# Two-layer hybrid block: gate logits from the attention product and from x, norm factors in the rows, gathers that add to the residual

## The chip, the cores and the metric

The kernel runs on one core of a Trainium2 chip. The metric is the device time of one launch in microseconds. Three runs of the kernel before took 533.31, 535.4 and 535.91 us, the median is 535.4. One more execution was taken with the hardware profiler; it is the source of every row shown below.

The engines have short names here. PE is the matrix engine (TensorE), and PEld its weight loads, which overlap the products. DVE is VectorE, ACT is ScalarE, POOL is GpSimd, and SP is SyncE, which issues most of the plain transfers. SBUF is the on-chip memory that all of them read, PSUM the accumulators that PE writes, DRAM the memory outside.

## The reference

The input is x, 16 sequences of 256 tokens with 128 features, 4096 tokens in all. Four sublayers add to it, each on a layer norm of x without scale or shift:

```python
x = x + attn_a(layernorm(x), ...)      # attention whose softmax is summed out
x = x + ffn(layernorm(x), gate_w, w1, w2)      # layer 1 of the experts
x = x + attn_b(layernorm(x), ...)      # selective scan
x = x + ffn(layernorm(x), gate_w, w1, w2)      # layer 2 of the experts
```

The first sublayer multiplies the softmax, summed over the axis along which it adds to one, by v of the same token. What remains is a linear map: v's projection, then the output projection, both with a bias.

The expert sublayer is a mixture of 8 experts. Each token takes the two with the largest gate logits (`x @ gate_w`), weighted by a softmax over these two logits; an expert is two products, 128 to 512 and back, with a relu between.

The selective scan has 16 states; it is computed for the last 180 tokens of a sequence and fewer for the faster states, and a test at the end of the kernel falls back to a general path where that would not be enough. The same test looks for experts that got more tokens than they have room for.

## The kernel before

**Tiles and stages.** Tokens are cut into 8 blocks of 512, each as four tiles of 128 tokens by 128 features (`x{b}`, tokens on partitions). Layer 1 takes the blocks in the sets [0], [1], [2, 3], [4, 5], [6, 7], layer 2 in the sets [0, 1], [2, 3], [4, 5], [6], [7]. For every set, `layer` (L1476) calls what comes before the experts (`attention`, L1024, in layer 1, `gate`, L1047, in layer 2), then `route` (L1139), then `experts` (L1189), then what comes behind (`arrive`, L1456, with the scan `mixer`, or `finish`, L1464, which writes the output).

**Attention and gate.** `attention` loads a block of the transposed input, transposes it on PE, copies it from PSUM to SBUF as x, takes mean and variance with `bn_stats` (`statistics`, L999), and adds the bias `batt` to x. The product of the transposed input with `wat` (the two projections in one, centred so that the mean drops out) is multiplied by the reciprocal deviation and added to x. Then `gate` takes statistics of the new x, normalizes it into `xn` (`normalize`, L1007), transposes `xn`, copies it from PSUM into `xnT`, multiplies each of its four tiles by the 8 gate columns `gw_s`, and copies the logits out. `rstd_of` (L978) works out the reciprocal deviation with a power on POOL and one correction step on DVE.

**Routing.** `choose` (L1063) finds the two largest logits of each token and their weights `p`. `route` counts, with short bf16 products, which place each token gets in its expert's list, writes a row `xn * p` for each of the two experts (relu and both products are positively homogeneous, so the weight can go in first), and scatters the rows with indirect transfers from POOL to `slots` in DRAM: 8 scatters of 128 rows for a block.

**Experts.** SP fetches an expert's rows (`xs`), PE transposes them, multiplies by `w1_s`, ACT or DVE take the relu (`h`), PE multiplies by `w2_s` (`ps_y`), the result is copied out (`yr`) and SP stores it to `ys` in DRAM. When all experts of a set are stored, `collect` (L1244) gathers for each tile its two rows by indirect transfers from POOL (`gather`, L866) into buffers `yy`, and DVE or POOL add them to x, 512 columns at a time.

**The order of the work.** All of this is first recorded as jobs (`Plan`), not issued. Each job has its possible engines and an assumed duration on each, an assumed time from issue to landing for transfers (`late`), and what it has to follow. `forward` (L299) walks through the jobs and gives each an engine and a place; a long string, `ORDER` (L50), holds the rank of every job and decides between those that are ready. The engines then get their instructions in that order, and each works through its own queue without overtaking. Where the walk leaves PE without work for half a microsecond or more, `tile_layers` puts filler products in (L1502, blank by ones, one per 0.26 us of assumed idle), which keep PE running. Between two scatters that go out one behind the other, POOL gets a small memset (L1508).

**Buffers.** PSUM has three one-bank buffers of the kind `b`, one of the kind `y` and two of two banks each of the kind `B` (`BANKS`, L48). In SBUF there are three buffers for the transposed input (`load_x`, L890), four for `xn`, three for rows and for `yy`. A reused buffer makes its next writer wait for its last reader.

In the profile, nearly every instruction has the line of one helper (L758, L752 in the changed kernel), so rows are told apart by the tiles that they name. Names in the profile leave out buffer numbers: `w_s` stands for `w1_s` and `w2_s`, `ps_b`, `ps_B` and `ps_y` for the PSUM buffers.

Of the kernel before, what the change touches and what calls it, by code (L numbers as in the profile page):

```python
# [19 lines left out]
P = 128  # L20
# [26 lines left out]
XN, ROW, XS, XT, H, YT, DEPTH = 4, 3, 4, 3, 4, 3, 3  # L47
# [3 lines left out]
    "c-lo*30#cp_kWj}DT#_AT7*zhQ6XChm91pS7A2IZi(Fe$gsvjHEQye<l%>^jvxkHdDbb>klt|mmyvzTbXS%<?d}iL6d7kr}^F815"  # L51
    "J?HU#VARmG%HBTCvo=}ry|n&yah-awiDRP9k+c_yjPV!WH?lfzanRb9_sVr|zjr;?vNb8P(*i|bF9&N++nrCm`^1`9mTCDLP(jsB"
    "akkpxLeF5E+<(H1gO}BR9C$XlUUA{epZqIz;hjflbGO<Wduz6~R2xewC3*Sgs~4>D>6&)gV94nOVcNnjhx$=(!^GzB!pI;03<_?R"
    "b!ah4eU<OA=EaTGQA>B^tzCM2dQh_KrJijwlKU0NO=o@&Nmq-lq<-2z2`f&H>b7HNp{;{FZO-eT7PY$`*$n=ir9n5ES-L%RE;mT1"
    "r+ewI2<#P;+?^ZNmd0j>1zyoPF|u;%Turs4g&7BijhVE}vB@npbge<&h_>mIJY^yJ*;a*5|4KKjIBV0jLqv$|ZQ|T#LDn%x3x9e4"
    ")vcl|DCecx=RWosPIG)als&WDIN{k5+3?db&K_F)sW0n{`$WdQ`SHtS|K1bnwnMikTOOaOvAsmlu|1U>;$7g^{p_#iW9GFhs0a2R"
    "y3a8>w?|uZ--f*j22;4Ov{}w3CqGnMg*0_osn>grZ{~B;{Y%!JzjMke;=bN)M{ic`=CMOVqutlp+JAfSw?%nccCWchmlzvGzgB3@"
    "ao#A~wDSJO`?Ed$D=((U%&*YxD!n$Y&l<nlaD%Iwo2%*h9XHIG^5OE$DWAtUd2~Ok@DG-B({;G8%jk*2-u;85vqx5$PQ7R`qs1$>"
    "CaAk%*pF=`M=$J*ZoF;xD#ALtX|S%%5YwSYA|i*DKEAvB$5EG<F|VwwLfbTsuFo!C((})Yl6!G)Hl-i`x+*5CT)WMrN^M%Qo9z9W"
    ">@-@t*g`lsXtuA>`o3naXO7dc$palSQwRFaS#%-t-uJHGyr!JfPs|J){jaC<!mKqByC)cIOlU1zXzua&hQrEuf1ln{-xtJ8DP8zp"  # L60
    "C*k(vUhLzSJKS#mEaaEA4YONPpr1f*t(^P(U|FE%r)XVw_3${~P_2HOcAB{jNiyoa=ic!`+bu`aPkpwq>^RH&)w4TO$4pGxc)hgW"
    "&u+yj)ZEgXolS>&jJrOxsO9OJ#L>QU!-Ll9jp!XWgBiPW-EP-&h1!)CLE|zq9`knEV=Jk*y!zz(%kxEAFRM=5c>I&6P2JX=k6(Fq"
    "WXaBZE}a9)BTl>P4?dDTVNk)%z`G_J<4upIrLA86B{m^`^Oe0$AD*7-blL1lOYV$MeeCkb&l%;qa&e8taoehK6Z#FBGym-4Gs}-^"
    "DE>~g9q}#x_qyqkLQ9Zy+SJLF%4E+`W5yPF?V9jsby>jsih7$d^GCgwm5#F4kqxmGww1h{mVHR<u1@W*n(H%e{G4-3DYL0U@#rhR"
    "FMAiP<pvps%=%u*w{jzw$a2?ZFLjB_A7VFpci7>jDLx-B-guL1n^!f*Z_s<!hvq)!q3eTVvtBL?Ut!@FKcuE*tkvlcgYRs)8+>ix"
    "%fq__53RRh`tQcJzBP8%a?zf6t|T|L_wba&DVd#D<a#;FrqAx{cy8N+Z<XB}ateQ6S!}AUKJ0Vj)*S0(n=Xc*uJ}Ivvt|GHV~I6d"
    "f_?D4^QC*IPrqgO)Q6q+rf$zI`y+l|M>m)Zyp-%VZE0TqGLKE#gI-x4JbAVu+rPpz;!MZ4<_As>SNxNF+A=6vGg)vwulB;D?@LX`"
    "^^<PvS-dyXdKm1!y{fQ}XJYD#x~SNO-S3JT9S+R3t~q9KcC+uSp9!(bPE&K7%CvrrEg7bK^KERHEJLuF(P`(u3j$M?)Zg9KYV!PE"
    "eyII1N^OyEj%Bs^zySdVe<#Ldu82NSeE-4li%m8zZ&%zf`8V5w3RLS7(iZbO>uec4&9m6it;i?IHP0tl$s8ZsDQndpbJsCLF17@j"
    "&0F8#H@mJ^Y|NKEGrpD&JKKx4(5bjJ$=vu-mb<~>GwN2((Z!LQ2Da874UN9v*?*5+*>KmaS!~cD9V_#ynB`yVUH^^tIG0zhZEZ3o"  # L70
    "XR@OHm)vaYqOuC#O|KjbuWre?mOr;^op;5kqDdP}y?XuhKC3zNj65t{cV|;vNmk&t34;5c7WXbk?nUV68TnjtoDqJiLRRGybn{_g"
    "p!d1$7Za|Jt9UJELtZt{8jv|^sFmY=>kMYm`vmU;#r6B2`^i#v`Jb@8<?3DjspD_mjKXW3dK!id6|1f8>se+N1@?K=cYwB4&&7wC"
    "-Ziqng6|i2a0?6MzI!*`4|_OlWAd)I>2_7s!HV$KZ~L4ajumKKogd-$@kY_4kO{rG5C49ONKU%_YpP8xr>=Kpq>-O(^xxOYhpioB"
    "-S&0lp~+U)?7|b)WX^rNAm-BNXQw>}UQKA4v}*m&IVFRgex7VtI^+%GEneZC=U#R&iE8X?@Nkj!uWQMpQnnon?lhMl@nvA=0?Tou"
    "mkrysCuDbzyo2+m8*R_6+&k0yRll(|v0~qvhw=J07NgA07~gOlZL`|!)U!(0#w~P*{jvxBC*BIWdpdbykdV-9Ve8bXpUmc|U(&qJ"
    "cMc>atsJp#K|{FShZg1HFS;QHZ8~|wUM>B0!8zI8Cb~5)gWFL%JM2}%_N+aBPRzX|7L<oR87^DzX%}PZ=yb|=^wKclMRxYMUYo1N"
    "1rKoPaCqp#nX7DLKc%#!YEmxal43Ux+4Pr@H=nDixUlGJVRD9Jzfp-!zeX&PJel?;q*Aj^ck<Dr@-L$XuW__monF%6?{3BZtF+d0"
    "HzQmGyW4pi%a)aDey+0ZaroDU1KR`Y6Z75OGOi?5<QnVNZU~4vdul?(wfd3w)QzX^GkEe&Z;5j8R@(vBdx_^Zn07a<=|6}ITBy-$"
    "*P>)Clgk<dO?!qd-m+vFeNH^<wje!<ayq!&_hih4?B+M4?9Np0jnJv~xIXUg<aqaw`EIn8#fvTGW|>~|I&A9jr1s#1VTsqZ(yq-`"
    "UZb3Bdz&y{-YQF1J$&^}wzee4!=Q_vv}2UxZ4>XNFpE?1@ACqZ-aM~<t*iCKIc$-y1~t?tBf=(WMv43P<h4Vj8{Ql<kd?8kQa`M|"  # L80
    "qc5i%O`mxgIb0Y}tl?dt7I(vMmRpJ6tYeXR-F7Wo+qL_>G2dzDWu}vjhgJn#(_XuxJjy@!?=|MV^cMC1vaW~E&EqeP=Et5)dHUAx"
    "<jv&ICXX6A<#1LTR_ron<U0Nh>(W1H+z8z?GT!>l3+vyZRv9DuPwStSbtwKzLTc;0u*s>POz6KO-7S~TsfmiZon?^lyROug>MAb3"
    "`)TL*SNYci$G6#xZ|<G+Bfh?G%~K77!Y*4<?QQCpg~Z2Byr7)w^7_i?+v)KUdp0b*U;X@;euZi2n0r?XJ~)^UpC`;-sj;kkD)Zw0"
    "#hzEPTl2Q8wYha$UcMzhApH1F`o_SiFWRoyM(%$6aB|_44JFmFgMN1F;+_0tXh0|H_aC=T9@AWDQnmQujQr}&UzOUg3WG&O!O`=r"
    "i7Vn_=7nVbe8i66qBEGEA>mfv8*788mnCvG^j%`Nnipl!FRI4$Tix?w=ElJEjsJM{*wo=pNa^TpiJJ5t&x4EC*Ur_odGaIj$<5^W"
    "Tf)k}$LhDPjM!xO?w?`dpT;lD+FM)rqqElgVb%r9J-@B1@hm7bHG0?m?x7*`7d_JM-B%jX9DVWHj)k>{AL?}e<=ybU?=AT~zt<zX"
    "S?x+u*Elq@<EI7gD}T)%8}Mptx0B)Vjb?QN_UOHcO8pjf$?95qL64sYPgJ~&Sdm|}Jih*;sif4|`-H=k=WB9`9cO;r;o7^luv_|r"
    "Qg%4!-#SezVb*TF=^=UV)(kuNk5)as%4oM@-QmKcjSd$zKAf-Y5K^FCbZ_ms#_CyHYoeFk=|AM0-L#ZRllHwcsu|PdcChfc_M`hc"
    "&tKP@Wv`tbDgF21(v>-JC7xSDdsNCE_x#E=@D3iSL)jMpsk4Uc_c}28*|XLr>RrIrjkNIypR@y);(J~mIjS}>%<EUY{@z2hcQzAe"
    "?-c3a)3xwp%6RYHrzbVWwLMc;pO|^pG3&^LJHmeR+P&xYXGVQJpStzA!{y+*BWgLa^!$;cCapP~ODU?`d@s|n(ICFR^_`FYo+HQa"  # L90
    "%{`=u$#t1{+vrz7&Az<UnIE#xzZkUJCHZ2MtnAjoC5>ZZol~jrW)>P|wjmE54Yw<){k&OjuBY9U$)+|xbUYFDgAR6`a^dkj!=zH~"
    "?(Kh)r=2tGsJDOPC$|B9*X{dF?kQxsSKO9Ad{=&CT<E;zW7ki8IpdmT?hUVw@&)e#AHOj)?)x}un)UL^jXGDG1IpyLZapcT+&X{h"
    "k*1~x?rO2UB1{*YZT%i}XlUTG_|KO%7#_CtTs41SMww5n_nXmQGj3k^{&L^sG-LU7dGxV?m7^bgnX&nZ|I1*LDu(IwD9rv@$TrXH"
    "w>d@UX9z}C8fjjuM}MC><zsKbzR$Yw?1?Tpr(;I){(-eeoBKb>?WdvJ=vGsdG@#kJCdKetzZKK}@yR*7tw#Uul|B7$e)bI9Tj??F"
    "^3UygON{=C)7%r_nyrkzo?;wvM!Jse^MF4vvTBwV<zjluFK}7IRp0ZH3pXyU{nM=UXe&$Wa>6@kmA}WXZ&wy9i@R%d;#X=``o!Xf"
    "1!*7O9ZRcNpLzPMTWp6(J(jqC9ud0FN5iW*wQ1baZkMvI4xc%t`|!}*o*tPWz9v<;|2kEEv3qVruZF4y?cO8I4h2v;vFfp-j{NoY"
    "smx$dT6EEx&9BufZmw_r*^RE=+`m^!n-iz|ai>XGw~cvGkuLX#{F#zFyJxFL{}y8t-!!9`X5(*M(S-y>=<^Ns-Gg1;)jeq1T6<%{"
    "hVV}MGp`==_nLGvTDaf!+uT7Xj2}3Aosl2@Qryu@y3K20q*Gz%hlb^^5{B&l**D)UFmT)MTtn$TY2?b=Yh3lO)tz3mi@l|F%-il@"
    "{*~PeI<mD*<-OyJxj*^mFTbol^TOyyw}75|28Hca|NWq$r(Vurt4D3$%NF(9{>SF^`^K5Zp=w_aJIDL(vvV4o_|mdTx64<L@aGqg"
    "c)lo#3|juSA}gQT;o{N7_kKm*ysDOoi4V`;bEj<kYc~ISdC(<hLFX;EFK_FjTfZj9JoNXVXO;FpFR1IBk}dXLG<VeEJkQ3f%f9Wr"  # L100
    "JzL*DVB^g=`+c(>Etq9m;IKR@u18qcE)F9Oy4|z<#N0Y@p^xs?yStvxPh&RFUs5ce1@81NxOnPP^X1uXP2-=P(QTS<o!IAFpLLft"
    "J1i4-I?JZ*DEhWv8g;3*rOYtZ(0A@lxlO@1?;`$d?xrL2G-F1n7kT$M-KqAD&42{I%SCYmEl-_ky1urmZnssbWyg5~bW)a-e;wTM"
    "h=re6TQba|e$t-<cSU>o8(+HED|Nb{`T4a>KmS8U+{eX2nb*JPZBpgwM&;8_YMZQGv?_o37^68eM$P>(*lx{*=A9qU(v5H5=vgn("
    "F{~5&^0Y!!S9Gk`smq^azsO&{$y>XK{!#8UME-c9_my+CPUUvr7fL!UyBQl-c5=4)<81}=FR_<i8}`}%P2cZ*msy`|RyOR*&FJ*m"
    "TP>(4x>rtzP0YR#n`N_BXBO`YQy*DfxnFT-cOT<LpCtWl-m|i$vs@IW*RBtG^l9W4Rw2*dal)xA`kvyQK}`IUT8g4XN~G~c<VA|%"
    "D4JnKhT|C}e8jKe2l7H5sP+e%qG=vJ2xJL^->QD3(3l|7_ys(WAIKJ}eU0h`mkF?l5e1fq(?tQd!+LyYcuJsD$1;MTdXOrG|2$Fs"
    "(E`KMG$&P3xQ7u`4&Z89Xx~l|oAAPNBDl+t?`hRZJk9d3nBi%aF&cLX6xkr4L$nAX3OtQlFdR6JVwD&)tl(9ypfxxeo&;6+uoNwV"
    "HF)MZnugCD!zck!5zeROH291*g?49QArHS%f&|eP@IQk`!yk)33+ONS1OJpA6avGD9Lp+buuLi8dy$1B0YO$!FsxDvrYQw@NYhFY"
    "&xTbTFNFtD32EifBBVx%doVdPdQQ=lDv2}=KC%MCau6RcN;p^q0n-e{AvM4j3ji^^2>z?cK-_~oh@6Cn9~gK8e<T8I-~<GlCi$ii"
    "Pt|EOgVdk^5rmp&Xuh3P@F);A!5)mBr=^?-iv>7}frXUHiXaid89<zqpbtFypr(`vj9ef=kOX2bSqj_|**1peBoL1%;RSf7;RKQ$"  # L110
    "APX!Jm5eG4=qUKbqX7Vw5rLDiidI0jMBKshJfq?^k0HRx6gtdf+IS!a1L*SzF`NLPNx)+TMaej|Hb|KO^n(}#j+Ss7xP?F?>uIG_"
    "6crLcQQ!bRR;HvmNFXewDLEJ?R3$Wn6LAlOp;U32;t8-)u!)Wcw36j1p2S5VfdqmW@D-BPUIY*iN7xS;f<%fGNAsMDz)BK7rb}Q5"
# [530 lines left out]
def tile_layers(  # L643
# [222 lines left out]
    def gather(out, in_, rows):  # L866

        def emit():
            nc.gpsimd.indirect_dma_start(  # L869
                out=real(out), out_offset=None, in_=real(in_),  # L870
                in_offset=bass.IndirectOffsetOnAxis(ap=real(rows), axis=0),
            )
# [102 lines left out]

    xs_, lg_, xn_ = {}, {}, {}

    def rstd_of(stats, n):  # L978


        def small(name):
# [591 lines left out]
```

## Time and profile before

| what | value |
|---|---|
| median of three runs | 535.4 us (533.31 to 535.91) |
| the profiled execution | 533.65 us |
| its span, first to last instruction | 531.8 us |
| PE busy | 500.7 us, 94% of the span |
| DVE, ACT, POOL busy | 335.4, 300.8, 313.3 us |
| mean granted PE clock | 0.995 |
| first expert rows reach PE | 52.2 us |
| last expert product's results leave PE | 508.7 us |
| indirect transfers issued on POOL | 128 scatters, 128 gathers |
| bytes moved by transfers | 54.04 MB |

A row of a group reads: line, engine, operation, output tile, input tiles, shapes, how many instructions; then busy time and mean length in ns of one; then how long the engine stood idle just before instructions of this group, and who ended most of that. An f32 product on PE shows as two instructions, a transpose as one. The busy time of PE counts overlapping instructions once, so it is less than count times mean. A row of the timeline gives start and length in us; the chain at the end goes back from the last instruction to what released it, step by step.

### The profile page before, as it was taken

What the parts mean: (1) busy time and instruction counts of PE and PEld (TensorE: products, weight loads), DVE (VectorE), ACT (ScalarE), POOL (GpSimd) and SP (SyncE); (2) the same over time, 40 slices, a digit from 0 to 9 for tenths busy, and PEclk for the clock granted to TensorE, in tenths of its full rate; (3) what the DMA queues carried; (4) which work ended last, traced back from release to release, by engine and by line L of the source; (5) the groups of instructions that cost most, each with busy time, mean ns of one, the idle gap of its engine ahead of it and who ended that gap; (6) DMA issues with size and microseconds to landing.
All of it is one profiled execution on the core that took longest, in us unless ns stands there. A gap on an engine that the chain in (4) does not pass through costs nothing. (4 is left out here: it accounts for less than half of the span.)

```text
span 531.8 us, 10149 instructions
## 1 busy us (share of the span) xinstructions
PE 500.7 (94%) x3480; PEld 426.2 (80%) x3480; DVE 335.4 (63%) x1059; ACT 300.8 (57%) x682; POOL 313.3 (59%) x428
## 2 busy tenths in 40 slices
PE   3999999999999999999999989999999999999993
PEld 3999899978877878787787767667877788999993
DVE  5666656568777865788968798687658555122201
ACT  1142646788668545886367965779653554355410
POOL 3438625877877473467712768726866773774332
PEclk9999999999999999999999999999999999999998
DMA  7992312324324332222321222242244432444121
GB/s 220 307 285 95 100 45 65 88 70 134 92 77 134 106 101 61 76 85 77 98 82 35 76 58 77 64 117 77 83 120 113 109 83 88 139 127 131 46 74 49
DMA packets 73930, 54.04 MB, mean 102 GB/s; under 512 B 7792, under 2 KB 66704, under 8 KB 73872
## 3 DMA queue, kind: packets, MB, share of 16 engines
q1 hardware_dynamic: 64016, 36.23, 24.0%
q0 software_dynamic: 8192, 16.79, 10.7%
q8 instruction: 29, 0.48, 0.4%
q10 hardware_dynamic: 1664, 0.29, 0.3%
q14 instruction: 29, 0.24, 0.1%
HBM read 26.53 MB, written 26.76 MB: 100 GB/s over the span
## 5 line engine op out<-in xcount | busy, mean ns | idle before, releaser
L869 POOL DMA_INDIRECT yy<-ys,of x128 | 126.5, 988 | 82.4 <-issue 39.0
L857 POOL DMA_INDIRECT slots<-row,to x128 | 127.5, 996 | 63.9 <-issue 22.3
L758 PEld LDWEIGHTS ps_y<-w_s,h 128*110 128x110 f32 (+1 forms) x1152 | 140.4, 179 | 20.0 <-issue 4.9
L758 PE MATMUL ps_y<-w_s,h 128*110 128x128 f32 (+1 forms) x1152 | 153.3, 275 | 1.0 <-ACT yr L758 0.9
L758 PE MATMUL ps_B<-xsT,w_s 128*128 128x330 f32 (+1 forms) x384 | 127.7, 458 | 3.2 <-DVE th L758 2.1
L758 PEld LDWEIGHTS ps_B<-xsT,w_s 128*128 128x128 f32 x384 | 65.8, 190 | 27.4 <-DVE th L758 2.3
L758 ACT ACTIVATE h<-ps_B 128x720 f32<-128x720 f32 (+1 forms) x74 | 55.4, 749 | 45.2 <-PE ps_B L758 42.4
L1502 PE MATMUL ps_y<-blank,ones_d 128*128 128x128 f32 x454 | 54.9, 277 | 1.7 <-DVE yr L758 0.7
L758 POOL TENSOR_TENSOR rstd<-var,root 128x8 f32<-128x8 f32 (+1 forms) x20 | 28.7, 1434 | 44.8 <-DVE var L758 43.8
L1502 PEld LDWEIGHTS ps_y<-blank,ones_d 128*128 128x128 f32 x454 | 52.5, 192 | 2.9 <-DVE yr L758 0.9
L758 PE MATMUL ps_b<-xsT,w_s 128*128 128x176 f32 (+1 forms) x256 | 51.8, 328 | 0.2
L758 PE MATMUL ps_y<-h,w_s 128*128 128x176 f32 (+1 forms) x256 | 51.2, 326 | 0.0
L758 ACT ACTIVATE h<-ps_b 128x400 f32<-128x400 f32 (+1 forms) x59 | 28.7, 486 | 25.4 <-PE ps_b L758 23.9
L758 PEld LDWEIGHTS ps_b<-xsT,w_s 128*128 128x128 f32 x256 | 40.7, 190 | 1.6 <-ACT h L758 0.4
L758 PEld LDWEIGHTS ps_y<-h,w_s 128*128 128x128 f32 x256 | 40.7, 190 | 1.5 <-issue 0.5
L758 ACT ACTIVATE th<-later,lneps,ha_s 128x112 f32<-128x112 f32 (+14 forms) x85 | 39.4, 502 | 0.0
L758 PE MATMUL ps_b<-ident,xs 110*128 110x110 f32 (+3 forms) x208 | 35.7, 260 | 1.4 <-DMA xs<-slots 1.2
L758 DVE TENSOR_TENSOR x<-x,yy 128x512 f32<-128x512 f32 x25 | 17.3, 690 | 28.7 <-DMA yy<-ys,of 28.7
L758 ACT ACTIVATE row<-xn,p 128x128 f32<-128x128 f32 x83 | 27.9, 392 | 10.5 <-DMA slots<-row,to 6.8
L758 ACT COPY yr<-ps_y 110x384 f32<-110x384 f32 (+1 forms) x33 | 15.8, 478 | 31.8 <-PE ps_y L758 31.6
L758 DVE BATCH_NORM_STATS2 stats<-x 128x6 f32<-128x128 f32 x128 | 30.2, 281 | 5.3 <-ACT x L758 5.0
L758 ACT ACTIVATE decay<-delta,nea 128x108 f32<-128x108 f32 (+13 forms) x85 | 31.8, 408 | 0.8 <-DVE delta L758 0.7
(175 smaller groups left out, 731.8 us busy)
## 6 DMA issues: line engine op xcount, KB each, us to landing
slots<-blank SPq DMA_DIRECT2D x3, 1536.0 KB
xs<-slots SPq DMA_DIRECT2D x24, 180.0 KB
ys<-yr SPq DMA_DIRECT2D x24, 180.0 KB
w_s<-in_w SPq DMA_DIRECT2D x16, 256.0 KB
xs<-slots SPq DMA_DIRECT2D x24, 165.0 KB
ys<-yr SPq DMA_DIRECT2D x24, 165.0 KB
xT<-in_xT SPq DMA_DIRECT2D x8, 256.0 KB
slots<-row,to POOLq DMA_INDIRECT x128
```

Of the source, the lines that this page charges most:

```text
L758: return lambda: f(*[real(x) for x in a], **{n: real(x) for n, x in k.items()})
L857: inst = nc.gpsimd.indirect_dma_start(out=real(out), out_offset=bass.IndirectOffsetOnAxis(ap=real(rows), axis=0), in_=real(in_), in_offset ...
L869: nc.gpsimd.indirect_dma_start(out=real(out), out_offset=None, in_=real(in_), in_offset=bass.IndirectOffsetOnAxis(ap=real(rows), axis=0),)
L1502: nc.tensor.matmul(out=spare, lhsT=ones_d.real(), rhs=blank.real(), start=True, stop=True,)
```

## The change

Layer 1's gate logits now come out of the attention product. `wat` grows from 128 to 144 columns: eight for the input's share of the logits (`centre` times `gate_w`) and eight for the attention's share (`wat` times those). `attention` writes the product into the wide PSUM buffers, adds the two shares (the second one times the reciprocal deviation) and a constant `bgw`, and has the logits but for one positive factor per token, which doesn't change which are the largest; `choose` multiplies the difference of the two largest by that factor ahead of the exponential. Statistics and the addition of `batt` read the transposed input out of PSUM; the copy of x is gone.

Layer 2's gate transposes x as it is and multiplies by the centred gate columns. In neither layer is there a normalized copy `xn` any more: the norm's factor and mean are multiplied into the two weights of a token (`rp`, `mp`), and a row is `x * rp + mp`.

In `collect`, a gather adds what it reads to x in the transfer itself (`compute_op`), so the buffers `yy` and the additions are gone, and the second gather into a tile has to follow the first. The planner assumes 2.2 us from issue to landing for a gather, where it assumed 2.0.

There are six buffers for the transposed input instead of three, and the string `ORDER` is another one, so that the order of the instructions differs on all engines from the first ones on. In PE's queue 201 filler products stand where there were 227: 115 ahead of the first expert rows (118 before), 30 among the experts' work (46), 56 behind it (63).

```diff
-XN, ROW, XS, XT, H, YT, DEPTH = 4, 3, 4, 3, 4, 3, 3
+XIN, ROW, XS, XT, H, YT, DEPTH = 6, 3, 4, 3, 4, 3, 3
@@ gather
                 in_offset=bass.IndirectOffsetOnAxis(ap=real(rows), axis=0),
+                compute_op=ALU.add,
             )
-        plan.job([("POOL", 1.26, emit, 2)], [out], [rows, in_], late=2.0)
+        plan.job([("POOL", 1.26, emit, 2)], [out], [rows, in_], late=2.2)
@@ weights
-    wat = new("wat", [P, P])
-    copy(wat, pw)
+    W = P + 2 * NE
+    wat = new("wat", [P, W])
+    copy(wat[:, 0:P], pw)
+    pw = bank("b", P, P)
+    matmul(pw, wvo, centre)
+    watT = new("wtmp", [P, P], bufs=3)
+    copy(watT, pw)
+    pw = bank("b", P, NE)
+    matmul(pw, centre, gw_s)
+    gwc = wat[:, P : P + NE]
+    copy(gwc, pw)
+    pw = bank("b", P, NE)
+    matmul(pw, watT, gwc)
+    copy(wat[:, P + NE : W], pw)
...
+    pb = bank("b", P, P)
+    matmul(pb, wo_s, bvw)
+    battT = new("wtmp", [P, P], bufs=3)
+    V.tensor_tensor(battT, pb, bow, ALU.add)
+    pb = bank("b", P, NE)
+    matmul(pb, battT, gwc)
+    bgw = new("bgw", [P, NE])
+    copy(bgw, pb)
@@ attention
             for t in range(NTT):
-                transpose(pt[:, ts(t, P)], xt[:, ts(t, P)])
-            known.append(copy(x.rearrange("p t d -> p (t d)"), pt))
-        r, _ = statistics(blocks)
+                transpose(pt[:, t], xt[:, ts(t, P)], hold=[x] if t == 0 else ())
+            for t in range(NTT):
+                V.bn_stats(out=st[:, i * NTT + t, :], in_=pt[:, t])
+            V.tensor_tensor(x, pt, batt.unsqueeze(1).to_broadcast([P, NTT, P]), ALU.add)
+        r = rstd_of(st, n, False)
         for i, b in enumerate(blocks):
             x = xs_[b]
-            product(x, x, batt.unsqueeze(1).to_broadcast([P, NTT, P]), ALU.add)
-            pa = bank("b", P, NTT, P)
+            pa = bank("B", P, 2, TB)[:, :, 0 : 2 * W].rearrange("p a (c w) -> p a c w", w=W)
             for t in range(NTT):
-                matmul(pa[:, t], xTs[b][:, ts(t, P)], wat, after=known)
+                matmul(pa[:, t // 2, t % 2], xTs[b][:, ts(t, P)], wat)
...
+            V.tensor_tensor(
+                z, pa[:, :, :, P + NE : W],
+                rr.unsqueeze(3).to_broadcast([P, 2, NTT // 2, NE]), ALU.mult,
+            )
+            V.tensor_tensor(
+                own, pa[:, :, :, P : P + NE],
+                bgw.unsqueeze(1).unsqueeze(1).to_broadcast([P, 2, NTT // 2, NE]), ALU.add,
+            )
+            V.tensor_tensor(own, own, z, ALU.add)
...
-        gate(blocks, 1)
+        rm_[1, blocks[0]] = statistics(blocks)
@@ gate
-        r, m = statistics(blocks)
...
-            xn_[b] = new("xn", [P, NTT, P], bufs=XN)
-            normalize(xn_[b], b, r[:, ts(i, NTT)], m[:, ts(i, NTT)])
-            xnT = new("xnT", [P, TB], bufs=3)
-            pt = transposed(xn_[b], xnT)
-            copy(xnT, pt)
-            lp = bank("b", P, NTT, NE)
+            xT = new("xnT", [P, TB], bufs=3)
+            pt = transposed(xs_[b], xT)
+            copy(xT, pt)
             for t in range(NTT):
-                matmul(lp[:, t, :], xnT[:, ts(t, P)], gw_s)
-            copy(lg[:, ts(i, NTT), :], lp)
+                matmul(
+                    lp[:, i * NTT + t, :], xT[:, ts(t, P)], gwc, hold=[lg] if i + t == 0 else ()
+                )
+        copy(lg, lp)
+        rm_[k, blocks[0]] = statistics(blocks)
@@ choose
+        V.tensor_tensor(p[:, 1], p[:, 1], r.unsqueeze(2), ALU.mult)
...
+        V.tensor_tensor(rp, p, r.unsqueeze(1).to_broadcast([P, 2, n]), ALU.mult)
+        V.tensor_tensor(mp, p, m.unsqueeze(1).to_broadcast([P, 2, n]), ALU.mult)
@@ route
-                        ("ACT", "activation", (r[:, t, :], xn_[b][:, t, :], AF.Copy), dict(scale=w)),
+                        ("ACT", "activation", (r[:, t, :], xs_[b][:, t, :], AF.Identity),
+                         dict(bias=m, scale=w)),
@@ collect
         for i in range(2):
-            y = new("yy", [P, NTT, P], bufs=ROW)
             for t in range(NTT):
-                gather(y[:, t, :], q.ys, q.of[:, i, lo + t : lo + t + 1])
-            product(xs_[b], xs_[b], y, ALU.add)
+                gather(xs_[b][:, t, :], q.ys, q.of[:, i, lo + t : lo + t + 1])
```

## The prediction

> **What bounds the kernel now.** I read the busy table first, then the windows of three stages, the groups by line, the order of the matrix engine (PE) in time, and the chain at the end. Of a span of 531.8 us PE is busy for 500.7, DVE for 335.4, POOL for 313.3, ACT for 300.8. The windows cut the span where the first expert rows reach PE (52.2) and where the last expert work leaves it (508.7); the columns are the stretch, its length, busy time and instructions of PE, PE's weight loads, DVE, ACT and POOL, then granted clock, DMA share and GB/s.
>
> ```profile
> 0.00:52.20 52.20, 42.26 (x342) 40.22 (x342) 32.70 (x174) 13.81 (x36) 26.24 (x70) 1.00 0.76 228
> 52.20:508.70 456.50, 443.53 (x3008) 371.49 (x3009) 301.09 (x883) 285.95 (x644) 279.54 (x351) 1.00 0.32 89
> 508.70:531.80 23.10, 14.87 (x132) 14.47 (x130) 1.61 (x3) 1.08 (x3) 7.56 (x8) 0.89 0.21 62
> ```
>
> In the 456.5 us between, PE stands idle for only 13.0: that stage is as long as PE's queue. Not all of the queue is work, though. Line 1502 puts filler products (blank by ones) where the order written beforehand expects PE to idle. Each f32 product is two instructions, so the 454 below are 227 fillers, of 54.9 / 227 = 0.242 us. By the program's order, 118 stand before the first expert rows, 46 in the long stage, 63 behind it. The groups that the change touches (busy us, mean ns of one, then idle before):
>
> ```profile
> L1502 PE MATMUL ps_y<-blank,ones_d 128*128 128x128 f32 x454 | 54.9, 277 | 1.7 <-DVE yr L758 0.7 <-ACT yr L758 0.6 <-DVE yT L758 0.4
> ...
> L758 PE MATMUL ps_b<-gw_s,xnT 128*128 128x8 f32 x128 | 16.7, 246 | 1.5 <-ACT xnT L758 1.5
> ...
> L758 PE MATMUL ps_b<-ident,xn 128*128 128x128 f32 x64 | 12.3, 280 | 1.1 <-DVE xn L758 1.0
> ...
> L758 PE MATMUL ps_b<-wat,xT 128*128 128x128 f32 x64 | 11.2, 311 | 0.9 <-DVE x L758 0.5 <-DVE wat L758 0.4
> ```
>
> The opening stage is a chain of small steps, with fillers in between. PE in order of time (start, length, what, count):
>
> ```profile
> 10.69 0.77 PE L758 MATMUL ps_b<-wtmp,centre 128*128 128x128 f32 x2 [3.55 <-issue]
> 11.85 2.92 PE L758 MATMUL ps_b<-wat,xT 128*128 128x128 f32 x12 [0.38 <-DVE wat L758]
> ...
> 27.75 1.06 PE L758 MATMUL ps_b<-gw_s,xnT 128*128 128x8 f32 x8 [0.23 <-ACT xnT L758]
> 28.66 2.92 PE L1502 MATMUL ps_y<-blank,ones_d 128*128 128x128 f32 x24
> ...
> 52.24 0.34 PE L758 MATMUL ps_b<-ident,xs 88*128 88x88 f32 x2 [0.73 <-DMA xs<-slots]
> ```
>
> The end is a chain with no PE work to hide it:
>
> ```profile
> 509.71 2.68 DMA ys<-yr
> ...
> 513.33 0.72 POOL yy L869
> ...
> 522.07 2.49 DMA yy<-ys,of
> ...
> 524.68 0.70 DVE x L758
> ```
>
> Eight gathers go out on POOL, one every 1.25 us (513.33 to 522.07); the last lands 2.49 us after its start, DVE adds, PE transposes.
>
> **The long stage.** I counted PE's program order of both kernels behind the first expert rows and cost each kind by its spacing in the trace. Eight gate instructions started at 27.75 and the next thing at 28.66: 0.91 / 4 = 0.228 us a gate product. Four transposes in a row are followed after 0.44: 0.11 each. A product with 128 columns takes 0.22, one with 176 takes 0.30 (eight instructions in 1.2), so one with 144, between them, 0.243.
> - Gate products 56 to 32 (layer 1's are gone, layer 2's stay): -24 x 0.228 = -5.5.
> - Transposes of x, xn and xT 88 to 60: -28 x 0.11 = -3.1.
> - Attention products: 16 of 128 columns become 8 of 144, the others having moved ahead of the stage: -3.5 + 1.9 = -1.6.
> - Fillers 46 to 30: -16 x 0.242 = -3.9. In the trace before, the fillers sit at 117 to 126, where PE waits for rows of blocks 2 and 3, whose gate products were only at 82 to 92 and whose scatters filled POOL at 100 to 120. Now these logits come with the attention product, before PE takes the first expert rows.
>
> The sum is -14.1, with the 13.0 us of idle kept as it was. By the groups' busy shares (0.26 a gate product, 0.19 a transpose of xn, 0.35 an attention product) it would be about -17.5: the far end. For the near end there is a rule that speaks against this step. The Trainium skill, "TensorE: Matmul & The Clock Gate", section "Back-to-back issue gap", puts the start-to-start floor of a narrow product at about 25 ns, where the trace has 114 ns an instruction. By that floor 24 gate products of two instructions are worth 1.2 us, not 5.5, and the stage gains 9.8. But every gate product's own weight load takes 190 ns in the trace, and the same section says that in a stream of load and product both set the spacing. I take the row.
>
> **The opening.** The wide weight (wat with two sets of gate columns) needs more small steps, one behind the other because they pass through one PSUM buffer: wat, its transposed twin, the bias, the bias for the gate, the first addition to x, the gate columns, two 8-wide products. Before, wat's product began at 10.69, its copy at 11.50, and what uses it at 11.85: 1.15 us a hop. wat can start at about 10.45 (ACT's first free moment, 10.13); three full hops bring the bias to 14.3, the addition of 512 columns (0.68) to 15.05, and the gate columns end at about 17.0. The attention products thus start some 5 us later than at 11.85. From there PE must work through, in order, 9.1 us of real work and 115 fillers (27.8 us), so the first expert rows come at 17.0 + 36.9 = 53.9, against 52.2: +1.7. What this covers: the routing of block 0 gets shorter (no second normalization, transposes, copy and gate ahead of it), its first scatter falls near 31.5 instead of 35.5 (POOL's row there), eight scatters and two powers later, some 13.3 us, its rows can be fetched at 46 and be there 3.1 us later (the spacing of 49.11 to 52.24 before), at 49. PE's fixed fillers are behind that by nearly 5 us, so the earlier routing gains nothing here; without that cover a late step would cost its own length. Ends: 0 to +4.
>
> On SP's queue two fills of 1.57 MB move ahead of most expert weights. Up to the last weight that is 9.2 MB; at the 248 and 293 GB/s of the first two 20 us, it is in by 35 us, and the third fill and two x loads by 42, before the first fetch at 46. It costs nothing.
>
> **The end.** DVE's addition with its two gaps goes (-0.96), and only the last of four transposes follows the last gather (-0.35). In their place is what an adding gather costs more, which no row shows. The nearest row is the plain gather: 0.95 us on POOL, 2.49 to land. Below, nothing more; above, POOL writing twice as much, 0.95 more for each, or 7.6 here. The descriptors name the same 128 rows of 512 bytes, so I stay near the plain row: +0.4 on the landing. Together -0.9.
>
> **The wait that is added.** Each of the 64 pairs of gathers now writes one x tile, so the second waits for the first; behind it on POOL stand the scatters and powers of the next set, and SP's fetches and PE's transposes wait for those. The Trainium skill, "DMA: Bandwidth & Descriptors", section "Rules for kernel authors", demands this: an accumulating DMA beside another access to the same bytes has to wait for the earlier one's semaphore. Were the pairs adjacent, that would be 2.49 - 1.25 = 1.24 us each, 79 us of POOL. In the program's order most partners are three POOL instructions or more apart (of the last eight: first with fourth, third with sixth, second with seventh, fifth with eighth), which is 3.75 us, longer than 2.49. Three pairs are adjacent, 3.7 us of POOL in all; two of them stand before the last blocks' gathers, where POOL idles 15.9 us for the ys store anyway. I count nothing.
>
> **What lies beside PE.** DVE loses 25 additions (17.3 us) and 29 normalizations (10.1), POOL 11 additions (13.9), ACT 35 normalizations (15.0) and eight copies of 0.59. The rows get dearer, since they take two factors: on ACT like the normalization, 482 against 389 ns, x82 = +7.6; on DVE 341 against 280, x46 = +2.8. Small DVE steps are added: 24 for logits, 30 for factors, at about 0.2 and 0.17. DVE and ACT each come out lighter; they were 63% and 57% busy beside PE, so this counts as zero; at full price it would be minus some ten each. Attention takes the wider PSUM buffers, which experts first use at about 100 us: no cost.
>
> **Sum.** 531.8 + 1.7 - 14.1 - 0.9 = 518.5 us of span. The profiled execution took 533.65, 1.85 more than its span: 520.4. The median of the runs shown, 535.4, is 1.75 above the profiled execution, so the forecast is 2.8% under the median.
>
> **Rivals.**
> - *Waits take the place of the work.* If the long stage is paced by what feeds PE, 14 us fewer instructions become 14 us more idle: 534.5, no change. For it: 46 fillers show that PE starves at places. Against: it idled only 13 us of 456, by many causes of at most 2 us.
> - *Less waiting too.* DVE, ACT and POOL are lighter, layer 2's logits no longer wait for a power on POOL (1.7 us) and a normalization; if PE's idle halves and the busy shares are the right price, another 6.5 + 3.4 go: 510.5. Against: weight loads waiting for "issue" are most of that idle, which the change doesn't touch.
> - *Slower: the adding gather is long on POOL.* If POOL needs d more for each, the end grows by 8d, and 16 gathers of blocks 0 and 1 stand among the scatters of blocks 2 to 5 (80 to 180 us, POOL busy 70 of 100 plus 0.3 between DMAs). It decides from 24d = 13.3, d = 0.55 us. At twice the plain time (0.95): +22.8, 543. Against: the same rows and bytes.
>
> **How the numbers follow.** Chances: the sum above 0.60 (own range 515 to 526), less waiting too 0.13, part of the gain lost to waits (526 to 532) 0.10, all of it 0.08, slower 0.09. A run tells 0.5% (2.7 us) from no change at best: faster 0.60 + 0.13 + 0.10 = 0.83, same 0.08, slower 0.09. The range 510 to 532 leaves out 0.08 + 0.09, and 0.03 below.
>
> **What would show it.** First expert rows on PE at 53 to 55, not at 45; the long stage near 442 with PE idle near 13; fillers at 201; the gather's POOL row near 0.95 and its landing under 3.7; 22 us at the end. I am wrong if PE's idle in the long stage passes 25, if the gathers' row is above 1.5, or if the attention products start after 21.

## The result, and the profile after

The changed kernel takes 585.85 us (580.7 to 586.68, four runs), the kernel before 534.95 beside it: a ratio of 1.093 (of the means), with a 95% interval of 1.089 to 1.098. The forecast was 520.4. The profiled execution has a span of 585.0, 53.2 more than before.

First the busy table, the granted clock in 40 slices and the software queue of the changed kernel. In the queue's line the columns are packets, MB and share of 16 engines' span.

```profile
PE 513.0 (88%) x3342; PEld 431.3 (74%) x3342; DVE 312.1 (53%) x1044; ACT 279.4 (48%) x620; POOL 385.3 (66%) x427
...
PEclk9999999899999979999999999999999979989795
...
q0 software_dynamic: 22528, 16.79, 15.8%
```

POOL gained 72 us of busy time (313.3 before), and it is the only engine beside PE that did; DVE and ACT each lost over 20. The software queue moved the same 16.79 MB, in 22528 packets instead of 8192. For 256 indirect transfers that was 32 packets each, on average. The scatters are as they were, so each adding gather brings 112 packets more: 144, if scatters and plain gathers have 32 each.

The groups of POOL's indirect transfers say where most of those 72 us sit (busy us, mean ns of one, then idle before), here the plain gathers of the kernel before, then the two groups of the changed kernel:

```profile
L869 POOL DMA_INDIRECT yy<-ys,of x128 | 126.5, 988 | 82.4 <-issue 39.0
```

```profile
L863 POOL DMA_INDIRECT x<-ys,of x128 | 201.8, 1577 | 85.7 <-issue 36.4
L851 POOL DMA_INDIRECT slots<-row,to x128 | 125.9, 983 | 61.2 <-issue 27.3
```

An adding gather holds POOL 0.59 us longer, 75.3 us in all; the scatters, which are as they were, take 0.98 (1.00 before). The rest of POOL's balance is other work that the change and its order moved on and off it. At the end of the kernel the same gathers stand one behind the other (start, length):

```profile
568.00 1.55 POOL L863 DMA_INDIRECT x<-ys,of  x1 [0.30 <-issue]
569.85 1.55 POOL L863 DMA_INDIRECT x<-ys,of  x1 [0.30 <-issue]
571.71 1.55 POOL L863 DMA_INDIRECT x<-ys,of  x1 [0.30 <-issue]
```

From start to start that is 1.855 us, where it was 1.25: 0.605 more for each, and 1.26 in the order's own accounting. From issue to landing the trace has a median of 3.3 us, where the last plain gather took 2.49. That time starts with the issue on POOL, so most of the 0.8 us more is the 0.6 for which POOL is held longer.

The windows of the three stages, cut at the same two events as before (first expert rows on PE, last expert work on PE):

```profile
0.00:58.30 58.30, 46.90 (x342) 43.53 (x343) 35.84 (x191) 8.26 (x24) 22.06 (x66) 1.00 0.72 214
58.30:556.20 497.90, 450.77 (x2886) 373.05 (x2885) 275.60 (x854) 270.23 (x594) 350.86 (x354) 0.96 0.36 81
556.20:585.00 28.80, 15.36 (x119) 14.76 (x117) 0.69 (x1) 0.96 (x2) 12.37 (x8) 0.74 0.24 47
```

The 53.2 us are +6.1 in the opening, +41.4 in the long stage and +5.7 at the end. In the long stage PE idles 497.9 - 450.8 = 47.1 us instead of 13.0. It is also busy for 7.2 us more, although it has 122 instructions fewer; the column behind POOL explains it, the granted clock is 0.96 where it was 1.00. Brought to the full clock, the busy time is 450.8 x 0.96 = 433 us (the clock has two digits, so 2 us either way), 11 less than the 443.5 before. So PE's work did shrink, by this estimate, and waits and a lower clock ate more than that: +34.1 of waits, -11 of work and +18 of clock make the 41.4.

What PE waits for is new as well. The waits of PE (sum in us, how often, the longest):

```profile
PE ps_b L752 <- DMA x<-ys,of: 24.8, 7, 7.6
PE ps_B L752 <- DVE th L752: 7.0, 5, 4.2
PE ps_B L752 <- ACT h L752: 6.6, 4, 3.5
```

The largest is the landing of gathers, which in the kernel before is not among PE's waits at all (there it was the additions' wait). Of these 24.8 us 17.1 fall in the long stage, so they are the largest single part of its 47.1 us of idle time, but less than half; the rest is spread over many waits, for DVE, ACT and other transfers. And the chain that ended last, followed back through the whole span, has one fifth of its length on one POOL line:

```profile
PE 46%; POOL 25%; DMA 12%; issue 11%; DVE 3%; ACT 2%; SPq 0%; ACTq 0%; POOLq 0%; DVEq 0%
POOL x L863 20%; PE ps_y L752 16%; PE ps_b L752 16%; PE ps_B L752 10%; DMA x<-ys,of 7%; PE ps_y L1547 5%; POOL slots L851 3%; DMA ys<-yr 2%; DMA xs<-slots 2%; DMA wo_s<-in_woT 1%; POOL rstd L752 1%; DVE red L752 1%; DMA na_s<-in_a_log 0%; DVE th L752 0%; DVE ps_B L752 0%
```

### The profile page after: what moved, and what is told of

Read it like the earlier page. It is cut to its first block, busy times and chain, and to the rows that moved or that the text cites. A ratio compares the mean times of both kernels' runs of the same rounds, so it can differ in the third digit from the quotient of the medians.

```text
span 585.0 us, 9757 instructions
## 1 busy us (share of the span) xinstructions
PE 513.0 (88%) x3342; PEld 431.3 (74%) x3342; DVE 312.1 (53%) x1044; ACT 279.4 (48%) x620; POOL 385.3 (66%) x427
## 3 DMA queue, kind: packets, MB, share of 16 engines
q1 hardware_dynamic: 64016, 36.23, 22.3%
q0 software_dynamic: 22528, 16.79, 15.8%
## 4 chain that ended last, share of the span: by engine, by line
PE 46%; POOL 25%; DMA 12%; issue 11%; DVE 3%; ACT 2%; SPq 0%; ACTq 0%; POOLq 0%; DVEq 0%
POOL x L863 20%; PE ps_y L752 16%; PE ps_b L752 16%; PE ps_B L752 10%; DMA x<-ys,of 7%; PE ps_y L1547 5%; POOL slots L851 3%; DMA ys<-yr 2%; DMA xs<-slots 2%; DMA wo_s<-in_woT 1%; POOL rstd L752 1%; DVE red L752 1%; DMA na_s<-in_a_log 0%; DVE th L752 0%; DVE ps_B L752 0%
## 5 line engine op out<-in xcount | busy, mean ns | idle before, releaser
L863 POOL DMA_INDIRECT x<-ys,of x128 | 201.8, 1577 | 85.7 <-issue 36.4
L752 PE MATMUL ps_y<-w_s,h 128*110 128x128 f32 (+1 forms) x1152 | 159.7, 282 | 4.0 <-DVE yr L752 2.0
L752 PE MATMUL ps_B<-xsT,w_s 128*128 128x330 f32 (+1 forms) x384 | 134.9, 475 | 10.1 <-DVE th L752 5.9
L752 ACT ACTIVATE th<-later,lneps,ha_s 128x112 f32<-128x112 f32 (+13 forms) x85 | 39.1, 503 | 2.6 <-DVE th L752 2.6
L752 ACT ACTIVATE h<-ps_b 128x352 f32<-128x352 f32 (+1 forms) x58 | 28.0, 483 | 23.3 <-PE ps_b L752 21.1
L752 DVE BATCH_NORM_STATS2 stats<-x 128x6 f32<-128x128 f32 x96 | 23.5, 282 | 28.4 <-DMA x<-ys,of 28.3
L752 PE MATMUL ps_b<-ident,x 128*128 128x128 f32 x64 | 13.7, 313 | 24.8 <-DMA x<-ys,of 24.8
L752 ACT ACTIVATE row<-x,mp,rp 128x128 f32<-128x128 f32 x82 | 34.6, 485 | 1.3 <-DVE rp L752 1.3
L752 ACT COPY yr<-ps_y 120x384 f32<-120x384 f32 (+1 forms) x32 | 15.3, 477 | 40.5 <-PE ps_y L752 40.3
L752 DVE COPY xsT<-ps_b 128x330 f32<-128x330 f32 (+3 forms) x30 | 13.8, 460 | 38.5 <-PE ps_b L752 37.9
```

Source lines behind the costliest of these rows:

```text
L752: return lambda: f(*[real(x) for x in a], **{n: real(x) for n, x in k.items()})
L863: nc.gpsimd.indirect_dma_start(out=real(out), out_offset=None, in_=real(in_), in_offset=bass.IndirectOffsetOnAxis(ap=real(rows), axis=0), ...
```

## The experiments

The theory (A) after this: the adding gather costs POOL 0.6 us more than the order counts on, and since each engine works through a fixed queue, that shifts what stands behind it on POOL until PE waits. The rivals: the rest of the change, or its new order, makes PE wait (B); the adding itself costs, through its later landing, its packets or the wait of the second gather for the first (C).

**The two halves of the change apart.** First, the changed kernel with plain gathers. The jobs are 32 more, so `ORDER` had to be written anew: a search of about 25 minutes over the ranks, by the kernel's own `forward`.

```diff
 gather:
-                compute_op=ALU.add,
...
-        plan.job([("POOL", 1.26, emit, 2)], [out], [rows, in_], late=2.2)
+        plan.job([("POOL", 1.26, emit, 2)], [out], [rows, in_], late=2.0)
 collect:
         for i in range(2):
+            y = new("yy", [P, NTT, P], bufs=ROW)
             for t in range(NTT):
-                gather(xs_[b][:, t, :], q.ys, q.of[:, i, lo + t : lo + t + 1])
+                gather(y[:, t, :], q.ys, q.of[:, i, lo + t : lo + t + 1])
+            product(xs_[b], xs_[b], y, ALU.add)
```

> The changed kernel with the gather part alone undone: gathers write the yy tiles again and 32 additions follow, everything else of the change stays; the order is written anew for the 32 jobs more. Theory A (the adding gather holds POOL 1.58 us instead of 0.99, in an order that counts on 1.26 with its issue, and every set's gathers stand ahead of work that PE waits for): 520 to 532, with the gathers' row back near 0.99, first expert rows still late at 57 to 59. Rival B (the rest of the change, or its order, makes PE wait): 565 or more with PE's waits still on the gathers or on DVE.

It took 531.75 us against 535.45 (ratio 0.9935, 0.9908 to 0.9962). Its gathers and its stages:

```profile
L861 POOL DMA_INDIRECT yy<-ys,of x128 | 125.0, 976 | 78.7 <-issue 33.9
```

```profile
0.00:58.00 58.00, 47.41 (x347) 43.55 (x348) 34.09 (x187) 9.32 (x27) 23.87 (x72) 1.00 0.71 216
58.00:508.00 450.00, 434.98 (x2931) 363.34 (x2930) 283.02 (x864) 277.43 (x612) 280.90 (x351) 1.00 0.32 90
508.00:530.30 22.30, 15.02 (x133) 14.59 (x131) 1.39 (x2) 0.96 (x2) 7.55 (x8) 0.88 0.17 49
```

Without the adding gathers the long stage has its clock of 1.00 and an idle time of 15.0 back, and is shorter than that of the kernel before. Rival B falls as far as the rest of the change goes; this kernel has an order of its own, so that the changed kernel's order is not at fault by itself has to come from the next runs. The opening is as long as in the changed kernel: its 6 us belong to the other half and its orders.

Then the mirror image, the kernel before with nothing but the adding gathers. The other jobs keep their order, ranked by their start in the order before.

```diff
 gather:
+                compute_op=ALU.add,
 collect:
         for i in range(2):
-            y = new("yy", [P, NTT, P], bufs=ROW)
             for t in range(NTT):
-                gather(y[:, t, :], q.ys, q.of[:, i, lo + t : lo + t + 1])
-            product(xs_[b], xs_[b], y, ALU.add)
+                gather(xs_[b][:, t, :], q.ys, q.of[:, i, lo + t : lo + t + 1])
```

> The kernel before with the gather part alone: gathers add into x, the 32 additions and the yy tiles go, the remaining jobs keep their order. Theory A: 128 x 0.59 us of POOL more, so 570 to 595, the gathers' row near 1.58, first expert rows at 52 as before. Rival B: the gather part is harmless alone, 525 to 540.

592.97 us, a ratio of 1.1096 (1.1041 to 1.1151): 57.5 us for this half alone. Its gathers' group, and the largest of PE's waits:

```profile
L831 POOL DMA_INDIRECT x<-ys,of x128 | 200.7, 1568 | 84.5 <-issue 37.2
```

```profile
PE ps_b L720 <- DMA x<-ys,of: 13.2, 7, 4.3
```

Since its order came by another rule than the one that it is compared with, that rule alone was tried on the kernel before, with no other edit:

> A control: the kernel before with its jobs ranked by their start in its own order, the rule by which the order of the kernel before with adding gathers was made. If that rule is harmless: 533 to 538. If it costs 5 or more, that much of the 57.5 us of that run is the ranking's and not the gathers'.

534.83 us, ratio 1.0001 (0.9984 to 1.0018). The 57.5 us belong to the gathers (with the yy tiles and the additions gone).

**POOL's time alone.** The kernel before, with plain gathers, the yy buffers and the additions, and a memset on POOL in front of each gather:

```diff
+    pad = sbuf.tile([P, 600], F32, tag="pad", name="pad")
     def gather(out, in_, rows):
         def emit():
+            nc.gpsimd.memset(pad, 0.0)
             nc.gpsimd.indirect_dma_start(
```

> The kernel before, gathers plain, with a memset of 600 numbers a partition on POOL in front of each gather (about 0.6 us by the row of the 724-wide memset, 0.70). No adding DMA, no wait of a partner gather, no more packets. Theory A: POOL's time alone does it, 570 to 595 and within 10 us of the kernel before with adding gathers. Rival C (what costs is the adding DMA's later landing, its 144 packets or the wait of the second gather for the first): 545 or less.

571.12 us, ratio 1.0698 (1.062 to 1.0777). The mechanism is there with no adding transfer at all, but it was 22 us short of the adding gathers, not within 10. Part of that is the dose, as POOL's timeline of this run at the end shows (start, length):

```profile
546.59 0.96 POOL L872 DMA_INDIRECT yy<-ys,of  x1 [17.04 <-DMA ys<-yr]
547.55 0.62 POOL L871 MEMSET pad<- 128x600 f32 x1
548.33 0.96 POOL L872 DMA_INDIRECT yy<-ys,of  x1 [0.17 <-issue]
```

From gather to gather it is 1.745 us, since behind a memset the gap ahead of a transfer is 0.17 and not 0.30. That adds only 0.495. So the dose was set to that of the adding gather, with 726 numbers:

> The kernel before with a memset of 726 numbers in front of each plain gather, so that one gather takes POOL 1.855 us from start to start at the end, as an adding gather does (the 600 of the run before gave 1.745). Theory A: the 35.7 us that 0.495 us a gather cost grow in proportion, 0.605/0.495 x 35.7 = 43.6, so 579; the 14 us up to the 593 of adding gathers are then the later landing and the wait for the partner. If POOL's time alone makes all of it: 588 to 598.

585.86 us against 534.7, ratio 1.0973 (1.0917 to 1.103), at 1.847 from gather to gather, 0.60 more. That is 51.2 of the 57.5 us. Neither number of the expectation was met: it lies between the proportional 579 and the 588 of "all of it". POOL's time, with no adding transfer anywhere, makes a price nine tenths as large; some 6 us, with an uncertainty of about 4 from the two intervals, are left for landing, packets and the partner's wait. They may be worth somewhat more than that: this run keeps the additions, seven of them on POOL (8.9 us), which the kernel with adding gathers is spared. Nor are the memsets quite POOL's time alone: DVE is busy for 344.4 us in this run, 9 more than before, with the same work. No run took rival C by itself; it is the smaller part.

The same memsets behind each gather instead of in front of it:

> The same 726 numbers, but behind each gather: POOL is held as long, every gather itself starts 0.73 us earlier. If the landing of a set's gathers is what PE waits for, this is shorter than with the memset in front by about 0.7 us for each of some 16 waits, 565 to 572. If only POOL's total counts: the same 579.

587.21 us, ratio 1.1005 (1.0948 to 1.1062). Each gather of its own starts 0.73 us earlier, and nothing is gained, where some 16 waits for landings would have given 12 us. So the landing by itself doesn't set the price; that leaves POOL's queue, in which everything later stands behind the added time.

Half of the dose, with 380 numbers (1.56 from gather to gather, 0.31 more):

> The kernel before with 380 numbers in front of each gather, about 0.30 us more of POOL. If every gather counts in proportion: 535.4 + 0.30/0.495 x 35.7 = 557. If there is slack and the price starts late (the prediction had only 24 gathers on the path, 0.30 x 24 = 7): 535 to 543.

553.27 us in two runs, ratio 1.0343 (1.0275 to 1.0411): +18.6. The 0 to 8 us of a price that starts late are ruled out; a small slack below 0.31 us is not, since nothing was run there. Set side by side, 0.31, 0.495 and 0.60 us a gather cost 18.6, 35.7 and 51.2 us, which is as if 60, 72 and 85 of the 128 gathers were on the path. The price rises faster than the dose.

Not all of that price is waiting. These three kernels have the very PE queue of the kernel before. Here is the long stage of the one with 726 numbers, cut at the same two events:

```profile
53.50:555.50 502.00, 457.58 (x3009) 378.28 (x3010) 310.07 (x883) 286.02 (x644) 365.73 (x472) 0.98 0.29 81
```

PE is busy for 457.6 us where it was 443.5, with the same products at a granted clock of 0.98 instead of 1.00; that is 14.1 us (10.3 and 10.7 with 380 and 600 numbers). The idle time in this stage grew by 31.5 us (9.6 and 22.4), and the end by 4.1 (2.5 and 3.7). Waits and the longer end alone are worth some 39, 53 and 59 gathers, still rising with the dose (the profile with 380 numbers is of the slower of its two runs, 556.13).

**Where the gathers count.** The kernel before with adding gathers in layer 1 alone; layer 2 keeps its yy.

```diff
         for i in range(2):
+            if q.k == 1:
+                for t in range(NTT):
+                    gather(
+                        xs_[b][:, t, :], q.ys, q.of[:, i, lo + t : lo + t + 1], compute_op=ALU.add
+                    )
+                continue
             y = new("yy", [P, NTT, P], bufs=ROW)
```

> The kernel before with adding gathers in layer 1 alone (64 of 128), layer 2 with yy and its additions. Gathers of layer 1 stand ahead of the mixer and of layer 2's routing, those of layer 2 mostly only ahead of the output and the next set: 570 to 580 (40 of the 57 us). If the two layers pay alike: 562 to 567. If, as the prediction had it, only the gathers of blocks 0 and 1 and the last eight count: 545 or less.

567.26 us, ratio 1.0607 (1.0572 to 1.0641): +32.6 for half of the gathers, 0.51 us each; the other half made up the remaining 25. I had expected 40 in layer 1. The layers pay more alike than that, 57% in the first, and the prediction's count of 24 gathers, which would have left it under 545, is far off.

**The order, written for the real price.** The changed kernel, adding gathers and all, with the planner told 1.86 us of POOL for a gather, and `ORDER` searched anew for that.

```diff
-        plan.job([("POOL", 1.26, emit, 2)], [out], [rows, in_], late=2.2)
+        plan.job([("POOL", 1.86, emit, 2)], [out], [rows, in_], late=1.7)
```

> The changed kernel with adding gathers as they are, but its order written anew with 1.86 us of POOL for a gather instead of 1.26 (and 1.7 to land instead of 2.2). Theory A with the loss in the order: 532 to 550, PE's waits for gathers mostly gone though the gathers' row stays at 1.58. If 75 us more of POOL cannot be placed beside PE by any order, or the adding DMA slows other engines: 570 or more.

548.06 us, ratio 1.0241 (1.019 to 1.0293): 38 us less than the changed kernel, with the same work on every engine but the fillers (43 more). Its long stage and its gathers:

```profile
56.30:518.30 462.00, 439.58 (x2931) 363.07 (x2930) 278.55 (x869) 270.59 (x589) 340.11 (x339) 0.99 0.38 86
```

```profile
L861 POOL DMA_INDIRECT x<-ys,of x128 | 203.0, 1586 | 70.6 <-issue 35.3
```

The gathers hold POOL as long as ever, 1.59 us each, and PE's idle time fell from 47.1 to 22.4. Most of the loss could be taken back by another order; the old one was written for a gather that POOL finishes in 1.26. That the true duration did it, and not a new search as such, is likely but not shown: the search wasn't repeated with 1.26, and 43 more fillers go with it. On the kernel before, a new search gave 3 us (below). The rest stayed: 16 us over the kernel with plain gathers (531.75), with 340 us of POOL work in a stage of 462.

**The opening.** The kernel with plain gathers, without any filler before 52 us of the written order:

```diff
-COLD = 12.0
+COLD = 52.0
```

> The changed kernel with plain gathers (yy and additions back) and no filler products before 52 us of the written order; nothing else moves. The prediction held that PE's fixed fillers, not the routing, set when the first expert rows reach PE. If so they come earlier than the 58.0 of the same kernel with fillers, at 52 to 55 (the fetch, now at 50.8, also moves up, since fillers stand ahead of the products of the routing), and the time is 526 to 530 instead of 531.8, unless the granted clock falls below 0.95 in the opening. If the rows' own chain sets it: still 57 to 58, and 531 to 534.

530.69 us, ratio 0.9923 (0.9895 to 0.995): the same as with fillers. The expert rows came at 58.6, not earlier. PE in order of time, and two windows of the opening:

```profile
43.52 0.26 PE L750 MATMUL ps_b<-both,onesb 128*128 128x32 bf16 x4
53.18 3.25 PE L750 MATMUL ps_B<-wat,xT 128*128 128x144 f32 x12 [9.40 <-DVE x L750]
...
58.60 0.32 PE L750 MATMUL ps_b<-ident,xs 88*128 88x88 f32 x2
```

```profile
40.00:53.10 13.10, 0.77 (x9) 0.50 (x8) 8.71 (x55) 3.61 (x9) 11.17 (x19) 0.55 0.17 60
53.10:58.60 5.50, 5.42 (x24) 5.39 (x25) 2.15 (x12) 0.00 (x0) 4.61 (x9) 0.53 0.27 94
```

Where the fillers stood, PE now waits 9.4 us for x. These are attention products of a later set; in this order they stand ahead of the first expert rows, and they need a PSUM buffer that DVE frees only after a power on POOL, and that stands behind the first eight scatters (48.47 in the timeline of POOL). The fetch of the rows went out at 49.7 and would have been there by about 53. The idle PE has also lost half of its clock: 0.55 and 0.53. The Trainium skill, "TensorE: Matmul & The Clock Gate", Part 1, says that the gate sets the clock by how busy PE has been of late; these two rows, with PE busy 0.8 us of 13.1, agree. So this run is no clean test of the fillers: my expectation had set aside a clock under 0.95 in the opening. At full clock the 5.4 us of products behind the wait would be 2.9, and the rows would come at about 56 (an estimate from these rows), still not at 52 to 55.

**What the rest of the change is worth.** The order of the first run with plain gathers came out of a short search. A sister of that search was carried on for 80 minutes more, the jobs unchanged:

> The changed kernel with plain gathers (yy and additions back) and an order searched longer than that of the first such run; the jobs are the same. If the change without the adding gathers is worth what the prediction gave it, and the first run of it (531.8) lost part of that in a rough order: 523 to 528. If its gain is the 0.65% already seen: 530 to 533.

527.18 us, ratio 0.9849 (0.983 to 0.9868), the fastest of all. As a control, the kernel before with its own order searched on by the same program:

> A control: the kernel before with its order searched by the same program for the same time. If a searched order alone makes a kernel faster: 528 to 531. If the gain of the run beside it comes from the smaller work: 533 to 536.

531.9 us, ratio 0.9948 (0.9927 to 0.997). That lies between the two cases of its expectation: a searched order alone gives half a per cent. It was searched for 40 minutes and not, as planned, for as long as the other, so the split is not exact; at most about 1% is left to the change without the adding gathers. The stages of the fastest kernel, cut at the same events (its profiled execution took 530.26 us, the longest of its five, 3.1 over the median):

```profile
0.00:58.20 58.20, 47.17 (x351) 43.89 (x351) 35.72 (x200) 10.14 (x29) 22.87 (x70) 1.00 0.70 212
58.20:505.70 447.50, 432.22 (x2888) 358.85 (x2889) 285.32 (x861) 273.85 (x599) 286.32 (x356) 1.00 0.32 90
505.70:528.50 22.80, 14.99 (x129) 14.40 (x127) 1.39 (x2) 1.54 (x3) 7.61 (x8) 0.85 0.20 59
```

## Why the prediction was wrong, step by step

**The step that failed: the adding gather taken near the plain row.** "The descriptors name the same 128 rows of 512 bytes, so I stay near the plain row: +0.4 on the landing." Both halves of that were off. The landing is 0.8 later (3.3 against 2.49), and most of that is POOL itself, which needs 0.605 us more for each gather; the sum had nothing for POOL. Same bytes did not mean same work: the queue's packets went up by 112 per gather. Of the prediction's three signs of being wrong, two came: a gathers' row of 1.58 (limit 1.5) and 47.1 us of PE idle time in the long stage (limit 25). The bound from both sides (0 to 0.95) held the value; what went wrong was to take the end nearest to the row of another kind of transfer, when no row showed this kind. The Trainium skill would have led the same way. "DMA: Bandwidth & Descriptors", section "Anatomy of one DMA — SWDGE (gpsimd) path", calls the writing of descriptors "small, variable" and says that many can be emitted before the cost shows. Here 112 more packets in a transfer go with 0.605 us more of POOL; the measurement decides. Whether the packets are the reason for the longer hold stays open.

**The second failure: how many gathers lie on the path.** The slower rival was this very mechanism, with the right sign. But it counted 24 gathers, the last eight and sixteen of blocks 0 and 1, and so put the point at which the gain is eaten up at d = 0.55; with memsets, 0.31 us already cost 18.6, more than the whole gain that was forecast. With d = 0.605 it gives 520.4 + 24 x 0.605 = 535, no change. The runs showed the price of 60 to 85 of 128, and of 39 to 59 when the slower clock is set aside. I had looked for windows in which POOL is nearly full, and taken the rest as slack. A likely reason why there was so little of it, argued and not shown: the order puts the work as tightly as its own durations allow, so what POOL loses reaches PE in most sets, and more so the larger the dose. Nine chances in a hundred for it were too few for a cost that no row showed.

**The third: idle time had no second price.** The sum kept the clock at 1.00 in the long stage. It fell to 0.96, which stretched 433 us of work to 451, about 18 of the 41.4 us. The memset run with 726 numbers shows it with nothing else changed on PE: the same products took 14.1 us longer. In the profiled executions of all kernels with more POOL time in an order not written for it the mean granted clock is lower (0.952 to 0.979 against 0.995; 0.991 with the rewritten order). That the idle time is the cause was not tried apart from it; the opening without fillers shows the clock following it.

**The long stage: PE's work was nearly right.** Forecast -14.1, to 429.4 us of work. The fastest kernel has 432.2 at full clock, with 33 fillers where 30 were counted (0.7 us): 11.3 less than before, 12.0 with equal fillers. The idle time kept at 13.0 was 15.3. A gate product holds its price: 8.5 us busy for the 32 that are left, 0.27 each, where the row before gave 0.26 and the floor that the prediction quotes would give two times 0.025. The stage comes out 9.0 us shorter, not 14.1, and that is 2.8 for the work and 2.3 for the idle time.

**The opening: the size off.** Forecast +1.7, measured +6.1, nearly the same with plain gathers (58.0). That PE's own queue sets it was right in the changed kernel: from 18.13 to 58.31 PE is busy for 38.7 of 40.2 us, and the rows, fetched at 50.84, would have been there at about 54 by the spacing of before. The terms were too small. The attention products began at 18.13 (forecast 17.0; the chain's first product came at 11.34, not 10.45, and three hops of 1.15 from 10.45 make 13.9, not 14.3). From there the 115 fillers took 27.5 us (forecast 27.8), the work between them 11.2 (forecast 9.1), waits 1.5 (forecast none): 4.4 us more in all than the 53.9 that were forecast. The routing's cover was thinner than thought as well. The first scatter was to start at 31.5 and started at 35.91. One link of that is a filler block; PE in order of time in the changed kernel:

```profile
22.95 9.65 PE L1547 MATMUL ps_y<-blank,ones_d 128*128 128x128 f32 x80
32.43 0.27 PE L752 MATMUL ps_b<-ident,wx_s 128*64 128x128 f32 x1
32.54 0.18 PE L752 MATMUL ps_b<-both,before 128*128 128x40 bf16 x1
```

`both` was ready at 29.75, and the counting product stood behind 40 fillers until 32.54. I had fillers down as what hides a late step; they can also make one late. How much that is worth is small: with plain gathers, the run without fillers has this product at 29.52 instead of 32.41, but its first scatter only at 38.36 instead of 39.47. And without fillers the first expert rows came no earlier, since other work of the same queue stood in the same place, at half the clock.

**The end and the added wait.** The end is 5.7 us longer with adding gathers, 8 x 0.605 = 4.8 of it as the rival had it; with plain ones, which have DVE's addition back, it is 22.3 and 22.8, against 23.1 before. The wait of a gather for its partner, counted as nothing, is 6.0 us of POOL in three waits in the changed kernel and 2.8 in four in the kernel before with adding gathers: small, as said. With the rewritten order it is 12.4 in eighteen, and may be part of the 16 us that this kernel is behind.

**The lighter engines.** DVE and ACT each lost over 20 us of busy time and nothing got faster by it, as said.

Put together for the fastest kernel, the stages make 58.2 + 447.5 + 22.8 = 528.5 us of span, against the forecast 518.5: 4.3 of the miss in the opening, 5.1 in the long stage, 0.6 at the end. That is the longest of five executions; by the medians the fastest kernel is 6.8 us over the forecast (527.18 against 520.4), so about a third of this miss is that execution's own.

## What to carry to other kernels

An operation with no row in the profile has no "nearest row" only because it moves the same bytes: give it its upper bound in the sum, or measure it alone, before anything is built on it. Where every engine works through a queue written beforehand, the price of a longer instruction is not its length times the few places that look full; here the whole price was that of half to two thirds of all of them, part of it through the lower clock that came with the waits, and an order rewritten with the true duration took back 38 of 51 us. An addition that DVE does in time that nobody waits for is cheaper than one that a transfer does in POOL's queue.

## What the runs showed that I had not expected

- An indirect gather that adds into SBUF holds POOL for 1.55 us, a plain one for 0.95 (medians), and brings 112 packets more.
- Behind a memset of 380 to 726 numbers the gap ahead of an indirect transfer on POOL is 0.17 us, behind another transfer 0.30.
- The cost of POOL time in this kernel rises faster than the dose: 18.6, 35.7 and 51.2 us for 0.31, 0.495 and 0.60 us a gather; 10 to 14 us of each is PE doing the same products at a granted clock of 0.98.
- Without fillers the granted clock was 0.55 from 40 to 53 us and still 0.53 in the 5.5 us of dense work behind it, and yet the kernel was no slower than with them.
